# One float32 weight for each edge in the last graph of a graph-attention kernel

## The chip, the core and the metric

The kernel runs on one core of a Trainium2 chip. The metric is the device time of one launch in microseconds (us), as a median of several runs. A profiled execution gives in addition a trace of every instruction on the core's engines: TensorE (PE, with its weight loads shown apart as PEld), VectorE (DVE), ScalarE (ACT), GpSimd (POOL) and SyncE (SP), whose queue issues the DMA transfers.

## The reference

There are 16 graphs of N = 1024 nodes with D = 256 features, and an adjacency matrix of zeros and ones with ones on its diagonal. Two layers follow each other, each with a residual and a layer norm:

```python
# layer 0: a gate per edge
e0 = leaky(einsum('bid,bjd->bij', h * a0, h))
x = layernorm(x + einsum('bij,bjd->bid', sigmoid(where(adj == 1, e0, -max)), h) + bias)
# layer 1: graph attention with H = 4 heads of F = 64
Wh = (x @ W).reshape(B, N, H, F)
e = leaky_relu(e_src[:, :, None, :] + e_dst[:, None, :, :], 0.2)
alpha = softmax(where(A > 0, e, -1e9), axis=2)
x = layernorm(x + elu(einsum('bijh,bjhf->bihf', alpha, Wh)))
```

e_src and e_dst are one number for each node and head: Wh times a_src and a_dst, summed over the 64 features. So the weight of an edge from i to j is exp(leaky_relu(s_i + d_j)), and a node's output is the sum of weight times Wh over its edges, divided by the sum of the weights. Column 65 of a sum holds those weights.

## The kernel before, in words

**Tiling.** A graph is cut into NB = 8 blocks of 128 nodes, and NH = 2 halves of 512 nodes (NQ = 4 blocks). In `stages` each step of a graph is a generator, and each `next` issues one piece of it. `issue` (L1229 and after) sorts the pieces of all 16 graphs by three tables of places, `FIRST`, `TIMES` and `LAST` (the first graph, the fourteen between, the last), shifted by `PERIOD` a graph, and issues them in that order, so each engine's queue is written out by hand: every engine takes its instructions in order. Two or three graphs are under way at a time. A place is an order, not a time on the clock.

**Layer 0** of a graph: `aload`, `cast`, `turn`, `mask` bring the adjacency (L267, L276, L291, L298; `mT` holds the mask as bytes), `xt`, `xtc`, `xta`, `score` (L356, `e`), `leak`, `leaky`, `sigmoid`, `below`, `lower`, `upper` make the gate, `agg` (L427) sums with it, and `moments` (L444, `st`), `gathered` (L450), `spread` (L468 and L469, on POOL), `shift` (L477) and `norm` (L489, for a few blocks L487) are the layer norm.

**Layer 1**, the part around the change. `yt` and `project` (L498, L517, `pw`) multiply by W and by the vectors a_src and a_dst, `wh` (L529) copies the result. `sources`, `rows` and `keep_rows` (L535, L541, L552, L553) write e_src to DRAM as rows, and `sload` (L648) loads a row of 512 numbers for a half and a head to all partitions, into `sbc` (four buffers). `top_dve` and `top_pe` (L560 to L591) find the largest e_dst of each head; the matmul `pbc` (L591) spreads it over the partitions and `tbc` (L575) copies it.

Now the weight of an edge is split into factors. Where s + d is at least 0 the weight is exp(s + d), elsewhere exp(0.2 (s + d)); after division by exp(s + top) the one is a factor of j alone, and the other a factor of j times rho, a factor of i. So:
- `exps` (L598 to L601) makes both factors of j and rho; `product` (L614 on ScalarE in the last graph, else L619) multiplies Wh by them; `high` and `low` (L633, L640) store these as fp32r numbers, a high part and what is left, side by side in `gm`: 2 x 130 columns for each head and block (64 + 64 for the two products, two columns for the weights' sums).
- `pos` (L658) makes, for each half, head and block of j, a 128x512 tile that is 1 where there is an edge and s_i + d_j is at least 0. Its pool has six buffers.
- `acc` (L670) multiplies this tile, 128 columns at a time as the stationary operand, by `gm`: 260 columns, 256 matmuls a graph. `acc_low` and `acc_sum` (L685, L693) add the two parts.
- `all_edges` (L705) turns the mask into fp32r, and `total` (L713, `tot`) sums over all edges, 264 columns, 128 matmuls a graph. `total_kept`, `total_less` and `weigh` (L749, L755, L780, L767 or L772) subtract the positive edges from all edges and multiply by rho.
- `divide` (L790 to L795, and L767 or L772), `elu` (L816), `join` (L807, L810) and the second layer norm end the graph; `leave` writes it. In the last graph, `weigh_end`, `divide_end`, `elu_end` and `join_end` (L826 to L867) do the last head of the second half apart.

**At the end** some checks of the value ranges (L1412 to L1427: `pmore`, `worst`, `bad`, `pm`, `good`, `flag`) decide if a general version, which covers other inputs, has to run. It doesn't here.

Of the kernel before, what the change touches and what calls it, by code (L numbers as in the profile page):

```python
# [19 lines left out]
SLOPE = 0.2  # L20
# [173 lines left out]
def stages(nc, k, pl, b, xg, adjg, outg, sums, span, zinv):  # L194
# [362 lines left out]
    def top_dve():  # L557
# [21 lines left out]
        cm = t["cm"] = small("cm", NB, H, bufs=1)  # L579
        nd = t["nd"] = small("nd", NB, H)  # L580
        nc.vector.tensor_tensor(cm, dst, tb, ALU.subtract)
# [25 lines left out]
    def product():  # L607
        for h, s in FACTORS:
            prod = t["prod", h, s] = pl.work.tile(
                [P, NB, F], F32, tag="sbc", name="prod", bufs=4  # L610
            )
            if last and s:
                for jb in range(NB):
                    nc.scalar.activation(  # L614
                        prod[:, jb, :], t["wh"][:, jb, h * F : (h + 1) * F], AF.Copy,
                        scale=t["es"][:, 1 - s, jb, h : h + 1],
                    )
            else:
                nc.vector.tensor_tensor(  # L619
                    prod, t["wh"][:, :, h * F : (h + 1) * F],  # L620
                    t["es"][:, 1 - s, :, h : h + 1].to_broadcast([P, NB, F]), ALU.mult,
                )
            yield
# [19 lines left out]

    def sload():
        for half, h in HEADS:
            sbc = t["sbc", half, h] = pl.work.tile([P, HALF], F32, tag="sbc", name="sbc", bufs=4)
            rows = t["sdram"].rearrange("(b h) n -> h b n", h=H)
            nc.sync.dma_start(  # L648
                out=sbc.rearrange("p (b n) -> p b n", n=P),
                in_=rows[h, half * NQ : (half + 1) * NQ, :].partition_broadcast(P),  # L650
            )
            yield
# [73 lines left out]
    def heads(half):  # L726

        return slice(0, H - 1 if last and half else H)

    def parts(half, pair, hs):  # L730

        u = t["u", half, pair][:, :, hs]
        return u[..., 0:F], u[..., F : 2 * F], u[..., 2 * F], u[..., 2 * F + 1]
# [40 lines left out]
    def weigh():  # L774
        for half, pair in PAIRS:
            ib, hs = half * NQ + 2 * pair, heads(half)
            u2 = second(half, pair)[:, :, hs]
            if half:
                ts = t["ts", pair][:, :, hs, 0 : F + 1]
                nc.vector.tensor_tensor(u2, ts, u2, ALU.subtract)  # L780
                yield
            times(u2, t["rho"][:, ib : ib + 2, hs])
            yield

    def divide():
        t["rz"] = small("rzs", NB, H)
        for half, pair in PAIRS:
            ib, hs = half * NQ + 2 * pair, heads(half)
            o, u2, z2, z1 = parts(half, pair, hs)
            nc.vector.tensor_tensor(o, o, u2, ALU.add)  # L790
            yield
            rz = t["rz"][:, ib : ib + 2, hs]
# [7 lines left out]

    def join():
        for half, pair in PAIRS:
            o, ex, _, _ = parts(half, pair, heads(half))
            yp = nodes(half, pair)[:, :, heads(half)]
            rows = (0, 1) if last and half else (slice(0, 2),)
            for q in rows:
                nc.vector.scalar_tensor_tensor(o[:, q], o[:, q], 0.0, yp[:, q], ALU.max, ALU.add)  # L807
            yield
            for q in rows:
                nc.vector.scalar_tensor_tensor(yp[:, q], ex[:, q], 1.0, o[:, q], ALU.min, ALU.add)  # L810
            yield

    def elu():
        for half, pair in PAIRS:
            o, ex, _, _ = parts(half, pair, heads(half))
            nc.scalar.activation(ex, o, AF.Exp)  # L816
            yield


    END = [(H - 1, pair) for pair in range(NQ // 2)]  # L820

    def weigh_end():
        for h, pair in END:
            if last:
                u2 = second(1, pair)[:, :, h]
                nc.vector.tensor_tensor(u2, t["ts", pair][:, :, h, 0 : F + 1], u2, ALU.subtract)  # L826
            yield

    def divide_end():
        for h, pair in END:  # L830
            ib = NQ + 2 * pair
            if not last:
                yield from (None for _ in range(4))
                continue
            rho, rz = (t[name][:, ib : ib + 2, h] for name in ("rho", "rz"))
            o, u2, z2, z1 = parts(1, pair, h)
            nc.vector.tensor_tensor(z2, z2, rho, ALU.mult)
            for q in range(2):
                nc.vector.scalar_tensor_tensor(
                    o[:, q], u2[:, q], rho[:, q : q + 1], o[:, q], ALU.mult, ALU.add  # L840
                )
            yield
            nc.vector.scalar_tensor_tensor(rz, z1, Z_MIN, z2, ALU.max, ALU.add)
            yield
            nc.vector.reciprocal(rz, rz)
            yield
            for q in range(2):
                nc.vector.tensor_scalar(o[:, q], o[:, q], rz[:, q : q + 1], None, ALU.mult)
            yield

    def elu_end():
        for h, pair in END:
            if last:
                o, ex, _, _ = parts(1, pair, h)
                nc.scalar.activation(ex, o, AF.Exp)
            yield

    def join_end():
        for h, pair in END:
            if not last:  # L860
                yield from (None for _ in range(2))
                continue
            o, ex, _, _ = parts(1, pair, h)
            yp = nodes(1, pair)[:, :, h]
# [5 lines left out]
    def leave():  # L870
        for half in range(NH):
# [5 lines left out]
            if half == NH - 1:  # L877
                nc.vector.tensor_tensor(zinv, zinv, t["rz"], ALU.max)
# [9 lines left out]
        top_dve=top_dve(), top_pe=top_pe(), exps=exps(),  # L888
        product=product(), high=high(), low=low(),
        sload=sload(), pos=pos(), acc=acc(), acc_low=acc_low(), acc_sum=acc_sum(),  # L890
        all_edges=all_edges(), total=total(), total_kept=total_kept(), total_less=total_less(),
        weigh=weigh(), divide=divide(), elu=elu(), join=join(),
        weigh_end=weigh_end(), divide_end=divide_end(), elu_end=elu_end(), join_end=join_end(),
# [7 lines left out]
PERIOD = 112.0  # L901
TIMES = {
    "xload": [-190.36],
    "aload": [-141.21, -134.94, -129.14, -126.41, -107.72, -95.92, -52.91, -49.35],
    "cast": [-133.33, -126.54, -110.85, -106.42, -72.33, -55.28, -40.89, -29.41],
    "turn": [-133.00, -118.97, -108.09, -86.35, -62.89, -45.14, -38.49, -26.07],
    "mask": [-126.25, -118.09, -94.06, -70.56, -52.12, -40.03, -32.69, -25.15],
    "setup": [-54.43, -50.76, -47.38],
    "xt": [-69.63, -66.83, -65.59, -61.38],
    "xtc": [-65.35, -64.69, -63.96, -57.76],  # L910
    "xta": [-60.02, -56.47, -53.23, -47.62, -40.80, -39.84, -35.73, -22.45],
    "score": [
        -55.95, -54.26, -52.86, -52.85, -50.30, -47.61, -41.77, -41.05, -37.61, -36.60,
        -31.53, -19.69,
    ],
    "leak": [
        -54.25, -52.28, -52.05, -51.99, -45.24, -41.19, -38.48, -36.59, -34.23, -28.07,
        -26.47, -19.19,
    ],
    "leaky": [  # L920
        -53.92, -51.61, -45.43, -45.41, -41.52, -40.38, -37.19, -36.20, -32.91, -26.88,
        -25.80, -17.05,
    ],
    "sigmoid": [-50.37, -36.56, -28.45, -23.28, -23.17, -15.81, -5.09, 4.38],
    "below": [-43.48, -40.73, -36.17, -28.75, -25.55, -24.80, -21.22, -11.11, 7.22, 7.95],
    "lower": [-41.97, -37.35, -33.23, -27.18, -24.41, -23.38, -19.01, -9.26, 8.37, 17.62],
    "upper": [-24.74, -21.21, -20.88, -18.06, 1.37, 12.57, 17.16, 22.61],
    "self_loop": [-22.52, -20.95, -18.10, -17.88, 3.26, 14.07, 18.13, 24.49],
    "agg": [
        -18.25, -16.27, -15.06, -15.02, -4.11, -4.03, -2.54, 0.32, 5.09, 8.13, 15.85,  # L930
        17.47, 21.46, 23.59, 23.78, 24.56,
    ],
    "residual": [-8.35, -7.46, -1.27, 2.37, 22.46, 22.48, 26.43, 27.74],
    "moments0": [-5.49, -4.53, 5.61, 8.01, 23.75, 25.11, 27.16, 28.13],
    "gathered0": [4.13, 6.42, 7.91, 10.51, 26.40, 27.32, 28.51, 29.05],
    "spread0": [13.40, 31.26],
    "shift0": [17.29, 31.54],
    "norm0": [21.66, 21.89, 22.47, 23.38, 34.53, 34.91, 35.50, 35.54],
    "yt": [27.46, 27.57, 36.68, 36.99],
    "ytc": [29.00, 29.33, 39.29, 39.57],  # L940
    "project": [32.52, 32.60, 33.90, 39.19, 40.28, 40.33, 40.41, 40.81],
    "wh": [33.22, 36.59, 37.58, 40.10, 40.68, 42.17, 42.34, 43.12],
    "sources": [41.16, 45.78],
    "rows": [41.83, 54.07],
    "keep_rows": [44.82, 56.53],
    "top_dve": [43.38, 45.01, 45.39, 50.81, 51.81],
    "top_pe": [44.42, 46.92],
    "exps": [51.81],
    "product": [53.02, 53.37, 53.98, 54.66, 58.34, 66.43, 69.20, 72.08],
    "high": [53.76, 54.40, 58.33, 58.56, 61.32, 68.49, 71.81, 73.63],  # L950
    "low": [54.19, 57.97, 61.74, 62.89, 71.04, 72.63, 75.29, 76.96],
# [526 lines left out]
```

## Time and profile before

| | |
|---|---|
| median of 3 runs | 1741.71 us (1741.22 to 1742.57) |
| span of the profiled execution (its own time, first to last instruction) | 1739.6 us |
| busy PE, PEld, DVE, ACT, POOL | 97%, 86%, 94%, 71%, 6% |
| one graph in the steady state | 104.4 us |
| last graph's `pbc` | starts at 1646.69 us |
| last `acc` matmuls | from 1716.81 us, 1.18 us |
| last `flag` | 1733.97 us |

The profiled execution has no time other than its span; the median of the runs is 2.1 us above it. Times in the text are us from the start of the span. A group of instructions is a line of the code, an engine, an operation and its tiles; `xN` is its count, then come busy us and the mean duration of one in ns, and the idle time of the engine before them with what ended it. A duration holds the latency, and the next instruction starts before it is over: the pace of a group is read from rows with several instructions in a row. Busy PE is modelled and overlaps.

### The profile page before, as it was taken

How to read it: one execution, taken by the hardware profiler on the slowest of the kernel's cores; microseconds unless marked ns; L12 is line 12 of the kernel's file. 1: busy time of each engine (PE TensorE's matmuls, PEld its weight loads, DVE VectorE, ACT ScalarE, POOL GpSimd, SP SyncE). 2: the span in 40 equal slices, each digit the busy share in tenths (PEclk: the TensorE clock that was granted, in tenths of full speed). 3: DMA queues.
4: the chain of work that ended last, by engine and by line, in shares of the span. 5: the costliest groups of instructions: out<-in, count | busy, mean ns of one | idle time of the engine just before them, and what ended most of it. 6: DMA issues, size and time to landing. Idle time of an engine off the chain costs nothing.

```text
span 1739.6 us, 29647 instructions
## 1 busy us (share of the span) xinstructions
PE 1692.1 (97%) x10580; PEld 1492.5 (86%) x10580; DVE 1639.6 (94%) x3663; ACT 1239.4 (71%) x2766; POOL 106.8 (6%) x138
## 2 busy tenths in 40 slices
PE   8999999999999999999999999999999999999984
PEld 5789898998979889898998979889898898979883
DVE  5498999999999999999999999999999999999998
ACT  7674957759587685967759587685967859586784
POOL 0000000010000101000010000101000010000100
PEclk9999999999999999999999999999999999999987
DMA  5542333434334343333435334443343424422020
GB/s 190 129 116 67 98 98 92 110 92 131 88 89 101 105 125 92 94 101 92 109 92 129 91 86 102 105 128 91 89 107 92 110 67 117 105 71 55 26 68 26
DMA packets 249005, 168.59 MB, mean 97 GB/s; under 512 B 133010, under 2 KB 232468, under 8 KB 248852
## 3 DMA queue, kind: packets, MB, share of 16 engines
q1 hardware_dynamic: 248848, 166.63, 36.1%
q8 instruction: 86, 1.41, 0.3%
q14 instruction: 67, 0.55, 0.1%
q10 hardware_dynamic: 4, 0.00, 0.0%
HBM read 118.10 MB, written 17.04 MB: 78 GB/s over the span
## 4 chain that ended last, share of the span: by engine, by line
PE 91%; DVE 3%; ACT 2%; DMA 1%; issue 1%; POOL 0%; SPq 0%; ACTq 0%; DVEq 0%; POOLq 0%
PE acc L670 27%; PE agg L427 24%; PE tot L713 14%; PE e L356 13%; PE pw L517 7%; PE pg L395 3%; PE pt L498 2%; PE pt L319 1%; DVE pos L658 1%; DMA sbc<-sdram 1%; ACT prod L614 0%; DMA aT<-a 0%; PE pbc L591 0%; ACT gm L633 0%; ACT y L489 0%
## 5 line engine op out<-in xcount | busy, mean ns | idle before, releaser
L658 DVE SCALAR_TENSOR_TENSOR pos<-sbc,nd,mT 128x512 fp32r<-128x512 f32 x1024 | 737.4, 745 | 10.5 <-PE acc L670 5.0
L670 PE MATMUL acc<-gm,pos 128*128 128x260 f32 x4096 | 608.6, 292 | 8.9 <-DVE gm L640 5.0
L670 PEld LDWEIGHTS acc<-gm,pos 128*128 128x128 f32 x4096 | 536.8, 190 | 19.8 <-issue 5.7
L427 PE MATMUL agg<-xb,gate 128*128 128x256 f32 x2048 | 463.5, 379 | 0.2
L427 PEld LDWEIGHTS agg<-xb,gate 128*128 128x128 f32 x2048 | 379.9, 190 | 47.6 <-DVE gate L419 1.2
L713 PE MATMUL tot<-gm,allm 128*128 128x264 f32 x2048 | 328.8, 297 | 5.4 <-ACT gm L633 4.9
L713 PEld LDWEIGHTS tot<-gm,allm 128*128 128x128 f32 x2048 | 281.4, 189 | 9.7 <-ACT gm L633 5.1
L356 PE MATMUL e<-xT,xTa 128*128 128x512 f32 (+3 forms) x768 | 264.3, 489 | 2.2 <-ACT xTa L344 1.4
L356 PEld LDWEIGHTS e<-xT,xTa 128*128 128x128 f32 x768 | 135.1, 191 | 106.4 <-issue 55.3
L685 ACT COPY low<-acc 128x260 f32<-128x260 f32 x256 | 89.8, 377 | 187.5 <-PE acc L670 187.3
L705 ACT CAST allm<-mT 128x512 fp32r<-128x512 uint8 x256 | 157.4, 615 | 33.4 <-PE tot L713 31.7
L489 ACT ACTIVATE y<-y,shift,rstd 128x256 f32<-128x256 f32 x254 | 136.3, 592 | 48.6 <-DVE shift L477 48.6
L276 ACT ACTIVATE a<-a 128x1024 bf16<-128x1024 int32 x124 | 131.3, 1059 | 32.1 <-DMA aT<-a 23.0
L298 ACT ACTIVATE mT<-aT 128x1024 uint8<-128x1024 bf16 x120 | 127.1, 1059 | 7.6 <-DMA aT<-a 7.5
L468 POOL TENSOR_SCALAR std<-mv 128x4 f32<-128x4 f32 x64 | 27.7, 432 | 1618.7 <-DVE mv L450 1447.1
L517 PE MATMUL pw<-w_aug,yT 128*128 128x264 f32 x512 | 121.8, 387 | 0.5 <-ACT yT L507 0.5
L376 DVE TENSOR_TENSOR gate<-e,gate 128x512 f32<-128x512 f32 x192 | 105.5, 556 | 14.5 <-ACT gate L368 14.4
L693 DVE TENSOR_TENSOR u<-acc,low 128x260 f32<-128x260 f32 x256 | 103.1, 425 | 10.5 <-ACT low L685 10.3
L444 DVE BATCH_NORM_STATS2 st<-y 128x6 f32<-128x256 f32 x256 | 107.5, 421 | 1.2
L517 PEld LDWEIGHTS pw<-w_aug,yT 128*128 128x128 f32 x512 | 93.4, 190 | 15.4 <-ACT yT L507 1.9
L368 ACT ACTIVATE gate<-e 128x512 f32<-128x512 f32 x192 | 90.2, 486 | 13.7 <-PE e L356 13.3
L412 DVE TENSOR_TENSOR gate<-gate,mT 128x1024 f32<-128x1024 f32 (+7 forms) x128 | 96.6, 755 | 2.9 <-ACT mT L298 2.4
(111 smaller groups left out, 1788.8 us busy)
## 6 DMA issues: line engine op xcount, KB each, us to landing
a<-in_adj_dram SPq DMA_DIRECT2D x124, 512.0 KB, 4.6
sbc<-sdram SPq DMA_DIRECT2D x128, 256.0 KB, 4.6
out_dram<-y SPq DMA_DIRECT2D x31, 512.0 KB, 3.5
xb<-in_x_dram SPq DMA_DIRECT2D x15, 1024.0 KB, 5.4
a_us<-in_adj_dram SPq DMA_DIRECT2D x4, 512.0 KB, 8.9
aT<-a SPq DMA_TRANSPOSE x120, 3.1
xb<-in_x_dram SPq DMA_DIRECT2D x2, 512.0 KB, 4.7
sdram<-srow SPq DMA_DIRECT2D x32, 8.0 KB, 1.4
```

The source lines that it names most:

```text
L276: nc.scalar.activation(t["a16", ib], t["a32", ib], AF.Copy, accum_out=sums[:, 0, at : at + 1])
L298: nc.scalar.activation(t["mT"][:, :, ib * P : (ib + 1) * P], t["aT", ib], AF.Square, accum_out=sums[:, 1, at : at + 1],)
L356: nc.tensor.matmul(e[:, 0:n], lhsT=t["xTa", jb][:, c, :], rhs=t["xT"][:, c, at : at + n], start=(c == 0), stop=(c == DC - 1),)
L376: nc.vector.tensor_tensor(ge, t["e", jb, at][:, 0:n], ge, ALU.max)
L427: nc.tensor.matmul(agg[:, 0:D], lhsT=t["gate"][:, jb, ib * P : (ib + 1) * P], rhs=t["xb"][:, jb, :], start=(jb == 0), stop=(jb == NB - 1),)
L444: nc.vector.bn_stats(st, t["y", half][:, q, :])
L489: nc.scalar.activation(y, y, AF.Identity, bias=shift, scale=rstd)
L517: nc.tensor.matmul(pw[:, 0:WD], lhsT=t["yT"][:, c, jb * P : (jb + 1) * P], rhs=k.w_aug[:, c, :], start=(c == 0), stop=(c == DC - 1),)
L658: nc.vector.scalar_tensor_tensor(p_, t["sbc", half, h], t["nd"][:, jb, h : h + 1], t["mT"][:, jb, half * HALF : (half + 1) * HALF], ALU.is ...
L670: nc.tensor.matmul(t["acc", half, h, q // 2][:, q % 2, 0 : 2 * E], lhsT=t["pos", half, h, jb][:, q * P : (q + 1) * P], rhs=pl.gm[:, h, jb] ...
L705: nc.scalar.copy(m_, t["mT"][:, j0 : j0 + 4, ib * P : (ib + 1) * P])
L713: nc.tensor.matmul(tot[:, 0 : H * F1], lhsT=t["allm", ib, jb // 4 * 4][:, jb % 4, :], rhs=pl.gm[:, :, jb, l, F:E], start=(jb == 0 and l == 0),
```

## The change

Only the last graph's second layer computes otherwise. The other graphs' layers hold the same instructions.

- With the largest e_dst (top) of the head taken out, the edge's weight is exp(0.2 (d - top)), which is a factor of j, times max(exp(0.8 (d - top)), exp(-0.8 (s + top))), times a factor of i that the division cancels. `exps_last` makes both numbers of j, `raise_last` the row's exponential in place in `sbc` (8 of 128x512, on ScalarE), and `pos_last` (L862) takes the maximum and multiplies by the mask, where `pos` compared and multiplied. Its tile is float32, no longer fp32r.
- `product_last` and `ends_last` make Wh times the factor of j, and the factor itself as column 65, in float32, in the place of an old `xb` and an old `a32` buffer (`fa`, `fb`).
- `acc_last` (L885) multiplies the tiles by these 65 columns: 256 calls, float32. For heads 1 and 3 of the second half its four results lie in four banks of another PSUM pool.
- `inverse_last` (L904, L905) and `scale_last` (L923) divide straight from PSUM, on VectorE and ScalarE; `elu_last` and `join_last` (L940, L947, L949) end the graph, in the second half with the last head apart.
- `high`, `low`, `acc_low`, `acc_sum`, `all_edges`, `total`, `total_kept`, `total_less`, `weigh` and `divide` have no place in the last graph's table any more; rho, `sd` and `nd` aren't made there. The `..._end` steps are gone.
- `FIRST`, `TIMES` and `LAST` hold new places for all steps, so the order of every graph on every engine and in SP's queue differs. `PERIOD` is the same.

The core of the diff (the tables are left out):

```diff
+        nc.vector.tensor_tensor(cm, dst, tb, ALU.subtract)
+        if last:
+            ntb = t["ntb"] = small("ntb", H, bufs=1)
+            nc.vector.tensor_scalar(ntb, tbc, SLOPE - 1.0, None, ALU.mult)
+            yield
+            return
...
+    def exps_last():
+        es = t["es"] = small("es", 2, NB, H)
+        for s, scale in ((1, 1.0 - SLOPE), (0, SLOPE)):
+            nc.scalar.activation(es[:, s], t["cm"], AF.Exp, scale=scale)
+        yield
...
+    def product_last():
+        for h in range(H):
+            nc.vector.tensor_tensor(
+                factor_of(h)[:, :, 0:F], t["wh"][:, :, h * F : (h + 1) * F],
+                t["es"][:, 0, :, h : h + 1].to_broadcast([P, NB, F]), ALU.mult,
+            )
+            yield
+
+    def ends_last():
+        for h in range(H):
+            nc.scalar.copy(factor_of(h)[:, :, F], t["es"][:, 0, :, h])
+            yield
...
+    def raise_last():
+        for half, h in LAST_HEADS:
+            sbc = t["sbc", half, h]
+            nc.scalar.activation(
+                sbc, sbc, AF.Exp, bias=t["ntb"][:, h : h + 1], scale=SLOPE - 1.0
+            )
+            yield
+
+    def pos_last():
+        for half, h in LAST_HEADS:
+            for jb in range(NB):
+                p_ = t["pos", half, h, jb] = pl.pos.tile([P, HALF], F32, tag="pos", name="pos")
+                nc.vector.scalar_tensor_tensor(
+                    p_, t["sbc", half, h], t["es"][:, 1, jb, h : h + 1],
+                    t["mT"][:, jb, half * HALF : (half + 1) * HALF], ALU.max, ALU.mult,
+                )
+                yield
...
+    def acc_last():
+        for half, h in LAST_HEADS:
+            for i in range(NQ if apart(half, h) else NQ // 2):
+                t["acc", half, h, i] = (
+                    bank("acc") if apart(half, h)
+                    else pl.ps_u.tile([P, 2, HALF], F32, tag="u", name="acc")
+                )
+            for jb in range(NB):
+                for q in range(NQ):
+                    nc.tensor.matmul(
+                        sums_of(half, h, q)[:, 0 : F + 1],
+                        lhsT=t["pos", half, h, jb][:, q * P : (q + 1) * P],
+                        rhs=factor_of(h)[:, jb],
+                        start=(jb == 0),
+                        stop=(jb == NB - 1),
+                    )
+                yield
+
+    def inverse_last():
+        t["rz"] = pl.small.tile([P, H, NB], F32, tag="rzs", name="rzs")
+        for half, h in LAST_HEADS:
+            rz = t["rz"][:, h, half * NQ : (half + 1) * NQ]
...
+                nc.vector.tensor_scalar(out, z, Z_MIN, None, ALU.max)
             nc.vector.reciprocal(rz, rz)
             yield
...
+    def scale_last():
...
+                    nc.scalar.activation(
+                        o[:, i, h * F : (h + 1) * F], sums_of(half, h, q)[:, 0:F], AF.Copy,
+                        scale=t["rz"][:, h, half * NQ + q : half * NQ + q + 1],
+                    )
+                yield
```

## The prediction

> **What bounds the kernel now.** I read the page's slices first, then the busy time by stage, then the groups. The slices (tenths of 40 equal stretches; PEclk is TensorE's granted clock):
>
> ```profile
> PE   8999999999999999999999999999999999999984
> DVE  5498999999999999999999999999999999999998
> ACT  7674957759587685967759587685967859586784
> PEclk9999999999999999999999999999999999999987
> ```
>
> TensorE and VectorE are both full from the third slice to the last two. The stages, as busy us (x instructions) of PE, PEld, DVE, ACT, POOL, then clock, DMA share and GB/s:
>
> ```profile
> 1430.00:1534.40 104.40, 104.40 (x659) 92.60 (x658) 102.18 (x227) 79.35 (x172) 6.60 (x8) 1.00 0.40 104
> 1646.70:1666.90 20.20, 10.06 (x56) 9.07 (x56) 20.07 (x45) 18.69 (x67) 0.00 (x0) 0.73 0.19 56
> 1666.90:1703.50 36.60, 36.57 (x287) 36.47 (x288) 35.73 (x71) 24.02 (x70) 1.69 (x2) 0.96 0.18 52
> 1703.50:1718.00 14.50, 10.69 (x69) 9.62 (x67) 13.84 (x27) 5.92 (x22) 0.00 (x0) 0.88 0.01 1
> 1718.00:1739.60 21.60, 0.37 (x1) 0.08 (x1) 13.94 (x67) 11.49 (x37) 2.64 (x4) 0.56 0.16 52
> ```
>
> The first row is one graph of the steady state: TensorE has no idle time, so there is nothing to win there, only to lose. What the change rebuilds is the other four rows, the last graph alone, after its `pbc` (1646.7): 20 us in which VectorE and ScalarE make the split factors and TensorE is half idle, 37 us bound by TensorE, 14.5 mixed, and 21.6 us after the last sum.
>
> **The price of one float32 pass.** What the last graph's sums cost now:
>
> ```profile
> L658 DVE SCALAR_TENSOR_TENSOR pos<-sbc,nd,mT 128x512 fp32r<-128x512 f32 x1024 | 737.4, 745 | 10.5 <-PE acc L670 5.0
> L670 PE MATMUL acc<-gm,pos 128*128 128x260 f32 x4096 | 608.6, 292 | 8.9 <-DVE gm L640 5.0
> L713 PE MATMUL tot<-gm,allm 128*128 128x264 f32 x2048 | 328.8, 297 | 5.4 <-ACT gm L633 4.9
> ```
>
> The means contain the latency; the pace stands in the chain of waits, where 4 acc take 0.48 us (0.120 each) and 4 tot 0.50 (0.125 each). Per graph acc has 256 and tot 128: 30.7 + 16.0 = 46.7 us. The new acc is float32 with 65 columns. The 1024 calls of agg and the 256 of pw stand as 2048 and 512 matmuls, so a float32 call is two passes, while acc and tot (fp32r) are one: 256 calls become 512 passes, and tot goes. No row has a pass of 65 columns. By streaming: agg's 24 matmuls of 256 columns take 5.18 us, 0.216 each, 0.84 ns a column: 55 ns. But each pass loads 128 weights:
>
> ```profile
> 181.59 0.90 PEld L319 LDWEIGHTS pt<-ident,xb 128*128 128x128 f32 x8
> 182.66 0.29 PEld L591 LDWEIGHTS pbc<-dtop,ones_r 4*128 4x128 f32 x2 [0.17 <-issue]
> 1698.45 0.32 PEld L1412 LDWEIGHTS pmore<-more,ones_r 128*128 128x128 f32 x2
> 4.80 1.57 PEld L319 LDWEIGHTS pt<-ident,xb 128*128 128x128 f32 x8 [2.51 <-DMA xb<-in_x_dram]
> ```
>
> pbc streams only 4 columns, and still its second load comes 0.29 - 0.18 = 0.11 us after the first; pmore, with 1 column, 0.32 - 0.19 = 0.13. The transposes run at (0.90 - 0.14) / 7 = 0.109. So a pass is bound by its load: I take 0.109, between 0.055 and 0.13. The sums cost 512 x 0.109 = 55.8 us, 0.872 per `pos` tile (8 passes): 9 us **more** TensorE work than now. The gain must come from elsewhere. (The fourth row is the same load at half clock, twice as long.)
>
> **What the change removes, adds and moves**, along the path, in the profiled execution's own time (span 1739.6; the runs' median is 1741.7, so 2.1 lies around it).
>
> 1. *Up to pbc.* The new queue holds 6 acc groups (0.48 each) of the graph before between pw and pbc, against 3, and 2 more before pw. pw ended at 1644.5; now 1645.5; then 6 x 0.48 gives pbc at 1648.4. No graph-14 matmul is left behind it (now five groups).
>
> 2. *The factors.* Removed: 8 products (4 as 32 ScalarE pieces of 0.24), 12 casts to gm, 12 low parts. After pbc (0.35) come tbc 0.2, cm and ntb 0.2, ScalarE two exps 0.3 and a copy 0.1, one 512-wide exp over sbc (`raised`, 0.6; ScalarE's 128x512 copies take 0.6), and pos. The sbc load must have landed: it lands some 6 us after srow's copy (write 1.4, load 4.6 by the page's DMA issues), near 1649.5, in time. SP's queue issues three sbc loads there; the fourth stands behind srow's second write and an output that waits for ScalarE, and is needed at 1676. First pos at 1651.0, first pass at 1651.7. Now the first sums of this graph start at 1654.7, and tot first finds its factors at 1666.9.
>
> 3. *VectorE sets the pace at first.* pos keeps its size; 8 in a row take 5.35 us:
>
> ```profile
> 1699.85 5.35 DVE L658 SCALAR_TENSOR_TENSOR pos<-sbc,nd,mT 128x512 fp32r<-128x512 f32 x8
> ```
>
> (5.35 - 0.75) / 7 = 0.66 each. The maximum and the F32 output I cost the same; no row shows them. In the new queue the first 24 pos share VectorE with the end of the graph before: ten 512-wide operations at 0.60 (two prod in 1.29 less 0.69), four st at 0.33, some 20 small ones at 0.08: 8.8 us. 24 x 0.66 + 8.8 = 24.6: at 1675.6. Then `inverse` of the third head waits for TensorE's last group (0.9) and takes 0.25; VectorE stands still, and pos 25 is queued behind it, so TensorE goes dry too: the passes of pos 25 start near 1677.8.
>
> 4. *Then TensorE does.* 40 pos x 0.872 = 34.9, and 1.5 where two joins and four st (4 us) outlast the buffers ahead: last sum at 1714.4. ScalarE's work fits: about 30 us in 65, and it loads its tables as often as before.
>
> 5. *After the last sum.* Now 21.7 us (1717.9 to 1739.6), because of low, acc_sum, weighing, dividing and joining two pairs of four parts. New: four clamps and a reciprocal 0.6, four scalings (0.24) and two exps on ScalarE 1.6, join 0.6, st and aggr 0.7: 3.5, then the same end, from POOL's std at 1730.2 to 1739.6: 9.4. Together 13. The end: 1727.4.
>
> 6. *The clock.* Between pbc and the first pass TensorE idles over 2 us. Windows of 3.4 us, the clock behind POOL's column:
>
> ```profile
> 75.50:78.90 3.40, 2.69 (x21) 1.95 (x19) 1.52 (x9) 3.21 (x7) 0.00 (x0) 1.00 0.33 62
> 1659.30:1662.70 3.40, 1.83 (x13) 1.41 (x11) 3.40 (x6) 3.40 (x10) 0.00 (x0) 0.99 0.09 26
> 1662.70:1666.10 3.40, 0.00 (x0) 0.00 (x0) 3.40 (x9) 3.40 (x14) 0.00 (x0) 0.51 0.63 194
> ```
>
> A window half filled (11 acc, then 2 us of nothing) was followed by half clock. So I count one such window: half of 3.4 us, 1.7. Span 1729.1, time 1731.2: **1731**.
>
> The Trainium skill's "TensorE: Matmul & The Clock Gate" (section "Why this matters for your kernels") asks only to avoid PE-idle gaps over about 3 us; by it the gap of 2 us would cost nothing and the sum would be 1729.5. The same page (section "PE-mode transpose") says transposes don't count as busy; the first row above is transposes nearly alone, and the clock stayed at 1.00. The trace decides against both.
>
> 7. *The tables.* The graphs 0 to 14 do the same work in another order. I cost that at nothing, because TensorE's queue covers what the others do; where an order is worse, it isn't covered, since VectorE has only 2.2 us to spare in 104.4. Bounds: -4 (TensorE idles about 8 us in the first 76.5) to +14 (1 us for each of 14 graphs).
>
> Of the 10.5 us gained, 8.7 come from the shorter end and 1.8 from sums that end sooner.
>
> **Rivals.**
>
> *The clock stays at half (slower).* At 65 columns the array streams 55 of every 109 ns, in the first stretch 8 x 55 of some 1030 per pos, 0.43. For full clock speaks the window of transposes, against it the window of 11 acc, which streamed 11 x 108 of 3400 ns, 0.35, and lost it. If streaming alone counts, the gap takes the clock and the narrow passes don't bring it back: the window from 1666.1, which did, streamed for about 2.7 us of 3.4. Then a pass is 0.213: 512 x 0.213 = 109, 1651.7 + 109 + 13 = 1774: time 1776. It decides once half clock lasts over 21 us, since each us of it costs a half.
>
> *The new order of the common graphs loses.* 0.75 us a graph makes 10.5 and eats the gain: 1742; 1 us: 1745.
>
> *A pass costs otherwise.* At 0.055 VectorE bounds to the end: 64 x 0.66 + 8.8 + about 7 from 1651.0, last sum 1709.8, time 1726.6 with the clock's 1.7. At 0.13 the 40 pos take 41.6, last sum 1721, time 1738.
>
> **How the numbers follow.** My forecast, with pass prices from 0.055 to 0.13 and the order within -4 to +3: 1722 to 1738, chance 0.62. The order costs over 5: 0.16, of which 0.07 is over 14 and so slower. The clock stays at half for over 21 us: 0.18, up to 1776; shorter spells lie between. Under 1722: 0.04. A measurement can tell 0.2% (3.5 us) from no change: faster is below 1738.2, slower above 1745.2. Faster 0.62 + 0.04 = 0.66, same 0.09, slower 0.07 + 0.18 = 0.25. Range 1721 to 1762: it leaves out the clock at half to the end and a gain at the start beyond the bound.
>
> **What would show it.** PEld on acc in the last graph, spaced 0.109, and x512. The last acc near 1715 and 13 us from there to the end. pbc of the last graph near 1648.4, and 104.4 us from each graph's pbc to the next, else the tables did it. PEclk in the last two slices: below 7 means the rival. Wrong would be a first pass after 1655, or TensorE idle for over 5 us between pos 25 and the last.

## The result, and the profile after

The changed kernel takes **1787.64 us** (median of 4 runs, 1786.89 to 1788.04) against 1741.47 us before (median of 4): 1.0261 times as long, 95% interval 1.0247 to 1.0274. The forecast was 1731, so its sign was wrong; what happened is the first rival, the clock that stays at half, which had a chance of 0.18 and a price of 1776.

The slices of the changed kernel's page, as for the kernel before:

```profile
PE   8899999999999999999999999999999999999896
DVE  5488999999999999999999999999999999999654
ACT  7675867768596775859678585967858686765411
PEclk9999999999999999999999999999999999999555
```

The first 37 slices look much as before. In the last three the clock is 5, while PE shows 8, 9 and 6: an engine that looks nearly full and runs at half speed. VectorE goes from 9, 9, 8 down to 6, 5, 4, ScalarE from 7, 8, 4 to 4, 1, 1: now they wait for TensorE.

The stages of the changed kernel, in the columns of before (us, then busy us and instructions of PE, PEld, DVE, ACT, POOL, then clock, DMA share, GB/s):

```profile
1440.00:1544.90 104.90, 104.45 (x652) 91.78 (x651) 102.33 (x226) 77.60 (x167) 7.56 (x8) 1.00 0.45 116
1653.80:1658.50 4.70, 1.51 (x13) 1.45 (x14) 4.33 (x11) 4.20 (x16) 0.00 (x0) 1.00 0.02 4
1658.50:1700.00 41.50, 39.35 (x184) 38.97 (x183) 23.49 (x52) 14.63 (x50) 2.02 (x2) 0.50 0.17 51
1700.00:1773.00 73.00, 69.55 (x323) 68.93 (x323) 38.29 (x80) 12.22 (x37) 2.02 (x2) 0.50 0.04 12
1773.00:1786.30 13.30, 0.37 (x1) 0.08 (x1) 4.94 (x22) 1.42 (x4) 1.26 (x2) 0.50 0.14 45
```

Row 2 is the first stretch after the last graph's `pbc`: a third busy. From 1658.5 to the end the clock is 0.50 without a break, 128 us. Row 4: 323 matmuls in 73 us are 0.226 each, twice the 0.109 of the forecast. Row 1 is one graph of the steady state, 104.90 us in place of 104.40, with 0.45 us in which TensorE is idle; there was none before.

Where the difference of the spans (1786.3 - 1739.6 = 46.7 us) arose:

| | before | after | difference |
|---|---|---|---|
| last graph's `pbc` starts | 1646.69 | 1653.75 | +7.1 |
| from there to the last `acc` matmul | 71.0 | 117.1 | +46.1 |
| from there to the end | 21.9 | 15.4 | -6.5 |

So the change did shorten the end, and lost seven times as much in the sums. Three lines of the changed kernel's timeline show where the loss starts (start, us, then the group; the bracket is the idle time before it and what ended it):

```profile
1656.39 3.40 DVE L862 SCALAR_TENSOR_TENSOR pos<-sbc,es,mT 128x512 f32<-128x512 f32 x5
1657.26 3.06 PEld L885 LDWEIGHTS acc<-fa,pos 128*128 128x128 f32 x19 [3.25 <-issue]
1657.29 3.00 PE L885 MATMUL acc<-fa,pos 128*128 128x65 f32 x18 [3.19 <-DVE pos L862]
```

TensorE was idle for 3.19 us before the first pass, until VectorE had made the first `pos`. The clock fell 1.2 us later. The first 11 passes started 0.109 to 0.112 us apart, the later ones 0.213 (median).

### The profile page after: what moved, and what is told of

The parts are those of the page before. It is cut to its first block, busy times and chain, and to the rows that moved or that the text cites. A ratio compares the mean times of both kernels' runs of the same rounds, so it can differ in the third digit from the quotient of the medians.

```text
span 1786.3 us, 29656 instructions
## 1 busy us (share of the span) xinstructions
PE 1751.4 (98%) x10708; PEld 1547.7 (87%) x10708; DVE 1636.5 (92%) x3624; ACT 1210.2 (68%) x2673; POOL 118.8 (7%) x138
## 4 chain that ended last, share of the span: by engine, by line
PE 83%; issue 12%; ACT 1%; DMA 1%; POOL 1%; DVE 0%; SPq 0%; POOLq 0%; DVEq 0%
PE acc L671 24%; PE agg L427 23%; PE tot L714 12%; PE e L356 12%; PE pw L517 6%; PE pg L395 2%; PE pt L498 2%; PE pt L319 1%; POOL rstd L469 1%; DMA a<-in_adj_dram 0%; DMA aT<-a 0%; ACT mT L298 0%; ACT a L276 0%; PE pbc L596 0%; POOL std L468 0%
## 5 line engine op out<-in xcount | busy, mean ns | idle before, releaser
L659 DVE SCALAR_TENSOR_TENSOR pos<-sbc,nd,mT 128x512 fp32r<-128x512 f32 x960 | 679.2, 744 | 8.2 <-PE acc L671 7.9
L671 PE MATMUL acc<-gm,pos 128*128 128x260 f32 x3840 | 585.5, 296 | 0.0
L671 PEld LDWEIGHTS acc<-gm,pos 128*128 128x128 f32 x3840 | 503.5, 189 | 23.7 <-issue 14.1
L427 PE MATMUL agg<-xb,gate 128*128 128x256 f32 x2048 | 474.1, 379 | 0.4 <-DVE gate L419 0.4
L714 PE MATMUL tot<-gm,allm 128*128 128x264 f32 x1920 | 308.6, 300 | 0.5 <-ACT allm L706 0.5
L714 PEld LDWEIGHTS tot<-gm,allm 128*128 128x128 f32 x1920 | 262.1, 189 | 10.5 <-DVE gm L638 4.2
L489 ACT ACTIVATE y<-y,shift,rstd 128x256 f32<-128x256 f32 x254 | 144.4, 598 | 119.0 <-DVE shift L477 77.0
L706 ACT CAST allm<-mT 128x512 fp32r<-128x512 uint8 x240 | 148.1, 618 | 73.3 <-PE tot L714 73.2
L686 ACT COPY low<-acc 128x260 f32<-128x260 f32 x240 | 81.8, 373 | 163.6 <-PE acc L671 162.9
L694 DVE TENSOR_TENSOR u<-acc,low 128x260 f32<-128x260 f32 x240 | 91.9, 419 | 6.8 <-ACT low L686 5.7
```

Source lines behind the costliest of these rows:

```text
L427: nc.tensor.matmul(agg[:, 0:D], lhsT=t["gate"][:, jb, ib * P : (ib + 1) * P], rhs=t["xb"][:, jb, :], start=(jb == 0), stop=(jb == NB - 1),)
L489: nc.scalar.activation(y, y, AF.Identity, bias=shift, scale=rstd)
L659: nc.vector.scalar_tensor_tensor(p_, t["sbc", half, h], t["nd"][:, jb, h : h + 1], t["mT"][:, jb, half * HALF : (half + 1) * HALF], ALU.is ...
L671: nc.tensor.matmul(t["acc", half, h, q // 2][:, q % 2, 0 : 2 * E], lhsT=t["pos", half, h, jb][:, q * P : (q + 1) * P], rhs=pl.gm[:, h, jb] ...
L706: nc.scalar.copy(m_, t["mT"][:, j0 : j0 + 4, ib * P : (ib + 1) * P])
L714: nc.tensor.matmul(tot[:, 0 : H * F1], lhsT=t["allm", ib, jb // 4 * 4][:, jb % 4, :], rhs=pl.gm[:, :, jb, l, F:E], start=(jb == 0 and l == 0),
```

## The experiments

Eleven kernels ran. "Narrow" is a pass of 65 columns as the change has it, "wide" one whose operand reads the same 65 columns twice, so that TensorE streams 130 in about the same time. A pass of 65 columns streams for an estimated 55 ns, by the 0.84 ns a column of agg's matmuls.

### Is it the streamed share that holds the clock? All passes wide

```diff
-                        sums_of(half, h, q)[:, 0 : F + 1],
+                        sums_of(half, h, q)[:, 0 : 2 * (F + 1)].rearrange("p (r f) -> p r f", r=2),
...
-                        rhs=factor_of(h)[:, jb],
+                        rhs=factor_of(h)[:, jb].unsqueeze(1).to_broadcast([P, 2, F + 1]),
```

> The changed kernel with each float32 sum streaming its 65 columns twice, 130 columns, the second copy unused; loads, passes and results as before. Theory (the clock follows the share of a window in which columns stream; 55 of 109 ns was too little to bring it back): a pass stays bound by its weight load, 0.111 us, the clock is back at 1.00 after one or two windows, last sum near 1657.3 + 62.7 + 1.7 = 1722, the time near 1737. Rival (weight loads are what the clock doesn't count, or float32 passes bound by loads run at half clock whatever they stream): 0.217 us a pass, 1787 to 1790.

Measured: 1739.13 us against 1742.01 before on the same chip, ratio 0.9985 (0.9975 to 0.9994). Twice the streaming, and 48 us less than the change. In these traces the clock changes only at whole multiples of 3413 ns from its other changes (to within 3 ns); the windows of 3.4 us below are cut there. The page's clock and the windows of this kernel:

```profile
PEclk9999999999999999999999999999999999999998
```

```profile
1653.79:1657.20 3.41, 0.64 (x5) 0.39 (x3) 2.84 (x9) 2.81 (x9) 0.00 (x0) 1.00 0.04 12
1657.20:1660.61 3.41, 3.00 (x14) 3.03 (x15) 3.41 (x6) 3.41 (x13) 0.00 (x0) 0.51 0.02 5
1660.61:1664.03 3.42, 3.42 (x32) 3.42 (x32) 3.39 (x8) 3.42 (x13) 0.00 (x0) 0.99 0.44 153
```

The same idle time before the first pass takes the clock here too. But 14 wide passes at half clock bring it back one window later, and it stays for 68 us. The weight loads, as many as before, are 0.111 to 0.112 us apart: the extra columns are free at full clock, since the load sets the pace. The theory held.

Nor does the length of a wait decide. In a later window of this kernel TensorE is idle for 1.54 us, and the next one is still at full clock:

```profile
1674.27:1677.68 3.41, 1.87 (x17) 1.68 (x16) 3.38 (x10) 0.93 (x4) 0.00 (x0) 1.00 0.43 113
1677.68:1681.09 3.41, 3.33 (x30) 3.14 (x30) 3.23 (x10) 0.00 (x0) 1.97 (x2) 1.00 0.05 14
```

The kernel below loses the clock after a window with a shorter wait, 1.26 us, between narrow passes.

### Is the idle time before the first sum to blame? Four unused matmuls in it

```diff
     def acc_last():
+        warm = bank("warm")
+        for _ in range(4):
+            nc.tensor.matmul(warm, lhsT=k.ident, rhs=t["yT"][:, 0, 0:HALF], start=True, stop=True)
```

> The changed kernel with four unused float32 matmuls of 512 columns (8 passes, 3.4 us) on TensorE between pbc and the first sum, so that the gap isn't idle. Theory, first form (the gap takes the clock, and 0.43 to 0.51 of streaming holds a full clock but doesn't restore it): clock 1.00 to the end, time near 1738. Second form (so narrow a stream loses the clock by itself): it falls one or two windows after the first sums, 1785 to 1790.

Measured: 1780.8 us, ratio 1.0224 (1.0207 to 1.0241). The time lies under the range of the second form and far from the first; the trace says something finer. Windows of this kernel, in the grid of its clock's changes:

```profile
1656.76:1660.17 3.41, 3.41 (x33) 3.41 (x32) 3.41 (x7) 3.41 (x12) 0.00 (x0) 1.00 0.02 5
1660.17:1663.59 3.42, 3.42 (x34) 3.42 (x33) 3.38 (x8) 3.42 (x15) 0.00 (x0) 1.00 0.45 153
1663.59:1667.00 3.41, 2.15 (x20) 2.01 (x19) 3.38 (x9) 2.08 (x8) 0.00 (x0) 1.00 0.00 0
1667.00:1670.41 3.41, 3.41 (x18) 3.41 (x18) 3.38 (x8) 2.70 (x10) 0.00 (x0) 0.50 0.02 6
```

Narrow passes without a gap (rows 1 and 2) **keep** full clock. In row 3 TensorE waits 1.26 us for a `pos`; 17 passes start in this window in place of 31, and the next one is at half. Then it never comes back, though TensorE is busy for the whole of row 4. So the gap before the first sum was only the first of several that could take the clock. This kernel, with that one filled, is 7 us faster than the changed one.

### Narrow after wide

If gap-free narrow passes keep the clock, a part of them can stay narrow. Three kernels widen only some of the eight groups of 64 passes (half and head), with `r` = 2 for those and 1 for the others:

```diff
+                    r = 2 if half == 0 else 1                # first four groups
+                    r = 2 if (half, h) == (0, 3) else 1      # the fourth alone
+                    r = 2 if half == 0 or h == 0 else 1      # first five
...
-                        rhs=factor_of(h)[:, jb],
+                        rhs=factor_of(h)[:, jb].unsqueeze(1).to_broadcast([P, r, F + 1]),
```

> The last graph's sums of the first half (256 passes) stream their 65 columns twice, so 130, those of the second half (256 passes) stream 65. The work is the reference's. Theory A: a window of 3.4 us keeps full clock as long as TensorE streams some 0.4 of it at full pace (lost: 17 narrow passes, 0.27, and 11 wide fp32r ones, 0.35; kept: 14 wide ones, 0.45, and 31 narrow ones, 0.50). Narrow passes without a gap, 0.111 apart, stream 0.50, and the second half has no gap over 0.7 us, so the clock stays at 1.00 to the last sum and the time is that of the run with all passes wide, 1736 to 1742. Theory B: a stream of narrow passes loses the clock by itself. Then it falls within two windows after the second half's first sum (near 1694), some 240 passes take 0.213 in place of 0.111, and the time is near 1763.

Measured: 1763.04 us, ratio 1.0119 (1.0101 to 1.0138): the number of theory B. But the premise of theory A, no long wait in the second half, was wrong, as the windows at the seam show:

```profile
1688.62:1692.03 3.41, 3.41 (x33) 3.41 (x32) 3.41 (x6) 0.17 (x1) 0.00 (x0) 1.00 0.23 67
1692.03:1695.44 3.41, 2.33 (x21) 2.14 (x21) 2.85 (x8) 1.96 (x6) 0.00 (x0) 1.00 0.05 15
1695.44:1698.86 3.42, 3.42 (x18) 3.42 (x18) 3.35 (x9) 0.00 (x0) 0.00 (x0) 0.50 0.00 0
```

Row 2 holds a wait of over a us, and 3 wide and 16 narrow passes start in it. This run alone tells nothing apart; the next two do.

> Only the fourth of the last graph's eight groups of sums (half 0, head 3) streams its 65 columns twice; the other seven are the changed kernel's. The work is the reference's. Theory A (a mark near 0.4 of full pace, below which a window loses the clock, and which narrow passes at half clock, 16 a window, 0.26 of full pace, cannot reach): half clock from about 1658 as in the changed kernel, back at 1.00 within 7 us of the fourth group's start near 1701, and kept after it: 256 narrow passes at 0.111 and some 32 wide ones at 0.111 in place of 0.213, 288 x 0.102 = 29 us less than 1787, so near 1758. Theory B (narrow passes lose the clock by themselves): it falls again within two windows after the group, some 9 us saved at most: 1778 to 1786.

Measured: 1756.26 us, ratio 1.0080 (1.0062 to 1.0099), as theory A had it (1758). The fourth group gets the clock back within two windows, and the narrow passes after it keep it to the end:

```profile
1701.55:1704.96 3.41, 3.41 (x18) 3.41 (x17) 3.39 (x6) 0.27 (x1) 0.00 (x0) 0.50 0.00 0
1704.96:1708.38 3.42, 3.42 (x33) 3.42 (x33) 2.41 (x5) 0.00 (x0) 0.00 (x0) 1.00 0.27 81
1715.20:1718.61 3.41, 3.02 (x27) 2.88 (x27) 3.38 (x9) 0.00 (x0) 1.21 (x2) 1.00 0.01 2
1722.03:1739.09 17.06, 17.06 (x156) 17.06 (x154) 14.96 (x30) 4.41 (x15) 0.00 (x0) 1.00 0.10 33
```

Row 1 is as busy as row 4 of the kernel with unused matmuls, at the same half clock, with as many matmuls (x18). On TensorE the one difference is 130 columns against 65, and here the clock returns. Row 3 is a narrow window with a short wait (25 passes start in it), and it keeps the clock; row 4 is 17 us of narrow passes alone at 1.00, 17.06 / 154 = 0.111 us each.

> The last graph's first five groups of sums (half 0, and head 0 of half 1; 320 passes) stream their 65 columns twice, the last three (192 passes) once. The work is the reference's. The run with four wide groups lost the clock in the window of 3.4 us at the seam, which held a wait of 1.35 us, 3 wide and 16 narrow passes (0.36 of the window at full pace). Theory A (a mark between 0.36 and 0.40 of a window): here that window is wide and keeps the clock, no later wait is over 0.7 us, so the last three groups run at 0.111 a pass to the end: 1737 to 1742. Theory B (narrow passes lose the clock by themselves, but slowly): half clock comes at the new seam or within the 21 us of the last three groups; from the seam it would be 192 x 0.102 = 19 us more, up to 1759.

Measured: 1739.39 us, ratio 0.9981 (0.9971 to 0.9991), theory A. The last three groups are narrow:

```profile
1700.20:1721.60 21.40, 21.40 (x194) 21.37 (x192) 18.13 (x41) 6.78 (x20) 0.47 (x1) 1.00 0.08 26
```

The windows side by side, with one of a later kernel ("one step moved"). The passes are those that start in a window of 3.41 us; the share is what they would stream at full clock (narrow 55 ns, wide 110, an fp32r pass of 260 columns 108 by the forecast; in the kernel before these come 218 ns apart at half clock, twice 109), over 3413 ns:

| kernel | window from | passes | share | clock in it | clock after it |
|---|---|---|---|---|---|
| changed | 1655.05 | 11 narrow | 0.18 | 1.00 | 0.50 |
| unused matmuls | 1663.59 | 17 narrow | 0.27 | 1.00 | 0.50 |
| before | 1659.33 | 11 fp32r | 0.35 | 1.00 | 0.50 |
| first four wide | 1692.03 | 3 wide, 16 narrow | 0.35 | 1.00 | 0.50 |
| one step moved | 1654.70 | 12 fp32r | 0.38 | 1.00 | 1.00 |
| fourth alone wide | 1715.20 | 25 narrow | 0.40 | 1.00 | 1.00 |
| all wide | 1674.27 | 14 wide | 0.45 | 1.00 | 1.00 |
| unused matmuls | 1656.76 | 31 narrow | 0.50 | 1.00 | 1.00 |
| changed | 1661.88 | 16 narrow | 0.26 | 0.50 | 0.50 |
| all wide | 1657.20 | 14 wide | 0.45 | 0.50 | 1.00 |
| fourth alone wide | 1701.55 | 16 wide | 0.52 | 0.50 | 1.00 |

One mark, between 0.35 and 0.38, fits every row, in both directions. Narrow passes have two stable states because of it: at full clock they come every 0.111 us and stream half a window, above the mark; at half clock every 0.213 us and, counted in work, a quarter, below it. Nothing that they do by themselves leads from the second to the first. That the clock follows just this is an inference, and the shares are estimates.

The table has eleven windows, and counting by starts can be off by a pass (0.03) at a window's edges. Counted over all 6643 windows of the thirteen traces, with each pass divided where a window ends (0.84 ns a column in float32, half of that otherwise), every window with a share below 0.36 was followed by half clock, and every one above 0.38 by full clock. Five lie between, and two of these kept the clock. So the mark holds far beyond the table, and is known to about 0.02.

### What the tables cost

Two kernels exchange them. The first is the changed kernel with the old `FIRST` and `TIMES`, the second the kernel before with the new ones; each keeps its own `LAST`.

```diff
 # changed kernel                       # kernel before
-FIRST, TIMES: new places              -FIRST, TIMES: old places
+FIRST, TIMES: old places              +FIRST, TIMES: new places
```

> The changed kernel with the first and the middle graphs' places (FIRST, TIMES) from the kernel before; the last graph's places stay. Theory (the new places cost what the last graph's pbc came later than I counted, 1653.8 against 1648.4): 1782, with 104.44 us from graph to graph instead of 104.90. Rival (the delay is the last graph's own): 1787 to 1788.

Measured: 1794.22 us, ratio 1.0302 (1.0285 to 1.0319).

> The kernel before with the new places of the first and the middle graphs; its last graph's places stay. Theory (the new places cost 5 to 7 us by themselves): 1747, 104.90 us from graph to graph. Rival: 1741 to 1742.

Measured: 1783.66 us, ratio 1.0239 (1.0222 to 1.0256).

Both times miss both theories, since places of one table and of another do not fit where they meet: the last interval from `pbc` to `pbc` is 117.2 us in the first kernel and 129.2 in the second, with single waits of TensorE up to 1.4 us in the first and 4.5 in the second. But between the seams both answer the question. One graph of the steady state, the changed kernel with the old places for all graphs but the last:

```profile
1123.25:1227.72 104.47, 104.47 (x658) 92.67 (x657) 102.25 (x227) 75.97 (x166) 6.61 (x8) 1.00 0.41 102
```

In the steady state most intervals are 104.44 to 104.47 us with the old places, whichever last graph follows, and 104.87 to 104.91 with the new ones, also in the kernel before. So the new places cost 0.45 us a graph there, and the last graph's code nothing.

Two tries to win it back failed.

```diff
 # TIMES: eleven steps moved, so that float32 and fp32r matmuls alternate less
-    total 0, 1: 77.28       acc 13: 90.48    total 15: 95.85   acc 16: 96.60
+    total 0, 1: 77.86       acc 13: 91.14    total 15: 96.77   acc 16: 96.77
-    total 26, 27: 125.51    acc 45: 139.12   agg 10: 19.18     below 6: -8.72   project 2: 38.80
+    total 26, 27: 125.60    acc 45: 139.56   agg 10: 20.66     below 6: -7.94   project 2: 39.52
```

> All of the last graph's sums stream twice, as in the run with wide passes (1739.1), and in the places of the common graphs ten steps are moved by up to 1.5 places so that TensorE goes nine times less a graph from float32 matmuls (gate, aggregation, projection, transposes) to fp32r ones (acc, tot) and back. The work is the reference's. Theory S: the new order costs 0.45 us a graph because TensorE changes kind 62 times a graph in place of 52, five round trips more, 0.09 each. Nine round trips less then give 0.8 us a graph: 104.9 falls to 104.1, and 14 graphs give 11 us: 1727 to 1731. Rival: the loss has another cause (steps that wait for other engines), or a moved step waits for its operand: 104.8 to 105.3 a graph, 1738 to 1745.

Measured: 1774.76 us, ratio 1.0191 (1.0177 to 1.0205); the interval became 107.77, worse than the rival had it. Theory S falls: the trace has 44 changes of kind a graph in place of 62, and yet new waits of TensorE: one of 1.37 us from a `tot` to an `acc`, one of 0.61 within `acc` and one of 0.42 within `tot` (what the starts are apart beyond the usual pace) are 2.4 of the 2.9 us lost. And these changes cost nothing anyway: from the last agg matmul to the second acc after it are 0.028 + 0.308 = 0.336 us, as much as one agg and one acc take (0.216 + 0.120), and from the last acc to the second agg 0.335.

```diff
 # TIMES: one step moved
-    project 3: 39.93      # behind the third and fourth transposes of y (39.52)
+    project 3: 39.511     # ahead of them
```

> All of the last graph's sums stream twice (1739.1 in the run with that alone), and in the table of the common graphs one step is moved: the fourth projection goes ahead of the third and fourth group of transposes of y, which in the new order wait 0.19 us for their operand from ScalarE in every graph. The work is the reference's. Theory W: the 0.45 us a graph that the new order costs are several small waits of TensorE, and this is the largest, so 104.89 falls to 104.65 to 104.75 a graph, and the time to 1736 to 1737. Rival: another wait takes its place and the interval stays at 104.85 to 104.95: 1739.

Measured: 1741.71 us, ratio 0.9995 (0.9986 to 1.0004). The interval is 105.2, not less but 0.3 more; the wait of 0.19 us before the transposes went, and one of 0.40 before the projection behind them came. Theory W got no support. What in the new places costs the 0.45 us a graph stays open. This kernel adds something on the clock: from `pbc` to the first pass are 3.5 us here too, but the idle time is split, 1.4 and 1.8 us, between two windows, and took nothing.

```profile
1654.70:1658.12 3.42, 2.01 (x17) 1.76 (x14) 2.45 (x12) 1.57 (x6) 0.27 (x1) 1.00 0.45 134
1658.12:1661.53 3.41, 1.63 (x14) 1.66 (x15) 3.41 (x6) 3.28 (x12) 0.00 (x0) 1.00 0.00 0
```

Either window is about half filled: 12 `acc` matmuls start in the first, 14 wide passes in the second. Where a pause falls among the windows is part of its price.

> As the run before, and in addition the four unused float32 matmuls of 512 columns between pbc and the first sum, which kept the first windows at full clock in the earlier run with them. The work is the reference's. Theory: no half clock before the last sum (the run with all passes wide had one window of it, 14 passes in place of 30), and the first group starts earlier; VectorE paces the first 24 tiles, so at most the 1.7 us of that window are won: 1734 to 1737. Rival: VectorE's pace eats all of it, or the unused matmuls delay the first sum: 1737 to 1739.

Measured: 1741.02 us, ratio 0.9988 (0.9979 to 0.9997), above what theory and rival had. Neither this kernel nor the one before had a half clock before the last sum, so the unused matmuls had nothing left to win, and the intervals of 105.2 stand against both.

The old places for graphs 0 to 12, the new ones for 13 and 14, all passes wide:

> All of the last graph's sums stream twice (1739.1 with that alone). The graphs 0 to 12 keep the places of the kernel before, 13 and 14 have the new ones. The work is the reference's. Theory: the new places cost 0.45 us for each graph in the steady state (104.89 against 104.44), so 11 intervals give 5 us back, and the one seam, between graph 12 and 13, costs what the two orders make each other wait: if it is below 2 us, the time is 1734 to 1736, faster than both kernels. Rival: the seam costs as much as the one between the old places and the new last graph did (its interval was 117.2 in place of 106.3): 11 us, so 1744 to 1746.

Measured: 1748.11 us, ratio 1.0035 (1.0021 to 1.0049), worse than the rival. The ten intervals after the first were 104.4 to 104.7 as expected; the two at the seam took 105.7 and 116.7.

The fastest versions are those with all passes and with the first five groups wide, 1739.1 and 1739.4 us. They are 0.15 and 0.19% below the kernel before. Their intervals leave out no change, but the gain is less than the 0.2% that the forecast named as what a measurement can tell.

## Why the prediction was wrong

**Step 6, the clock, failed.** It counted one fallen window, 1.7 us. The fall came where it was expected, with the pause between `pbc` and the first pass, but the clock stayed at half for all 128 us. The forecast took the passes' streaming at full clock (0.43 of a `pos` tile's time) for enough to win the clock back; at half clock they come half as often, and 16 a window reach 0.26. The rival had this right, 55 ns of streaming in each pass and "the narrow passes don't bring it back", and the kernel with wide passes shows it. The rival's doubt stayed because the forecast held a window of transposes for evidence that the narrow passes would do as well. But a transpose has 128 columns, 108 ns of streaming in a pass of 109, by the same 0.84 ns a column, where a narrow pass has 55.

The rival's price was 11.6 us short, which is in three other terms: the first pass came at 1657.3 and not 1651.7, the passes took 113.5 us and not 109, and the end 15.4 and not 13: 5.6 + 4.5 + 2.4 = 12.5 on an end of 1773.7, so 1786.2 of the measured 1786.3.

The other steps can be read off the kernel with wide passes, which kept the clock:

- **Step 7, the tables, nothing, with bounds of -4 to +14.** Measured +7.1 at the last `pbc`: 0.45 us a graph in the steady state (the first 13 intervals +4.6 in sum), +3.3 in the last two, -0.9 before the first. Inside the bounds, and on its bad side. The reason given, that TensorE's queue covers the others, was wrong by 0.45 of 104.4 us. For step 1 it means 1653.75 in place of 1648.4, 5.4 us more.
- **Step 2, first pass 3.3 us after pbc.** 3.5 in the changed kernel and in this one. Right.
- **The price, a pass at its load's pace, 0.109.** 0.111 to 0.112 at full clock, wide or narrow. Right within 3%.
- **Step 3, the tile behind the first 24 starts 26.1 us after the first pass.** 28.2. TensorE waits for a `pos` three times (1.08, 1.54 and 1.21 us) where the forecast named one wait.
- **Step 4, the other 40 tiles in 36.4 us.** 37.7. (The forecast's own terms give 1677.8 + 36.4 = 1714.2 for the last sum, where it wrote 1714.4.)
- **Step 5, 13 us after the last sum.** 15.0 from the start of the last matmul, of it 5.0 to POOL's std and not 3.5, and 9.9 from there and not 9.4. Two lines of the kernel with wide passes:

```profile
1724.06 0.53 DVE L949 SCALAR_TENSOR_TENSOR y<-u 128x384 f32<-128x384 f32 x1
...
1728.51 0.23 POOL L468 TENSOR_SCALAR std<-mv 128x4 f32<-128x4 f32 x1 [25.89 <-DVE mv L450]
```

Between these stand the rest of the join in two halves, four `st` and four `mv`, one after the other on VectorE; the forecast had put 0.6 and 0.7 us for them.

So with the clock held, the change is worth 7.4 us of loss up to the last `pbc` against 8.6 us of gain behind it, 1738.4 against 1739.6 in the spans. With the last `pbc` where the forecast had it (1648.4, 5.7 us sooner) the span would be 1732.7 against the forecast's 1729.1; this is worked out, and no kernel shows it, since each mixture of tables paid more at its seam than it won. What remains, 3.6 us, is mainly steps 3 to 5, each 1.3 to 2.1 us short, less the 1.7 us of step 6, since the one fallen window of this kernel lies within step 3.

**The rule on the clock.** The Trainium skill's "TensorE: Matmul & The Clock Gate", section "Why this matters for your kernels", asks to avoid idle gaps over about 3 us. Here a gap of 1.26 us in a stream of narrow passes was enough. Its section "What's actually happening" gives full clock after one busy window of about 3.4 us. The width agrees (3413 ns between clock changes); "busy" does not, if it is read from the busy time: windows with 3.41 of 3.41 us busy stayed at half until the columns of each pass were doubled.

## What to carry to other kernels

When an edit makes matmuls narrower than their weight load, work out how much of a 3.4 us window they stream at half clock too: if that is below the mark, one pause locks the kernel at half speed, and "PE 9" in the slices hides it, so the clock row is to be read first. Such passes are load-bound, and streaming 130 columns in place of 65 cost nothing here at full clock. Not all have to be widened, but those around the waits: one group of eight won back 31 of the 48 us, the first four 25, the first five all. Here each mixture of two tables of places lost more at its seam than the new table cost as a whole; a table is best kept or replaced as a whole, and its price read from one interval of the steady state, not from the total time.

## What the runs showed of the hardware

- Doubling the columns of a float32 pass with 128 loaded weights from 65 to 130 left its pace at full clock at 0.111 to 0.112 us, and took 48 us off the kernel.
- At half clock both take the same too: 0.213 us narrow, 0.215 wide.
- A change from float32 matmuls to fp32r ones, or back, cost nothing measurable (0.336 and 0.335 us for a pair that takes 0.336 us by its paces).
- The granted clock followed the share of a 3413 ns window in which TensorE streams columns, counted at full pace: below 0.36 half clock came next, above 0.38 full clock, however busy the window was (estimated shares, all windows of thirteen traces).
